# Adding b2 to x with accumulating DMAs in the main loop of a cross-attention and FFN kernel

## The chip, the cores and the metric

The kernel runs on one core of one Trainium2 chip. A core has TensorE (PE; matmuls, with a row of its own, PEld, for weight loads), VectorE (DVE), ScalarE (ACT), GpSimd (POOL) and SyncE (SP), which here only issues DMAs, and 16 DMA engines. The engines run side by side and wait for each other through semaphores; each works off its own queue in order. The metric is the device time of one execution in microseconds. Before the change the median of 3 runs is 529.81 us (529.16 to 530.25).

## The reference

The inputs are x of 4 x 2048 rows of 512, a context of 154 rows per batch, and weights. What matters of the reference, shortened:

```python
x = x + xattn(layernorm(x), ctx, Wq, Wkv, Wout, bout)
x = x + ffn(layernorm(x), w1, b1, w2, b2, gamma, beta)

def ffn(x, w1, b1, w2, b2, gamma, beta):
    h = layernorm(x) * gamma + beta
    h = qlinear(h, w1, b1)
    h = gelu(h)
    return qlinear(h, w2, b2)

def qlinear(x, w, b):
    xq, sx = act_quant(x)      # rows to integers in -128..127
    wq, sw = weight_quant(w)   # the matrix to -1, 0, 1
    return xq @ wq.T / (sx * sw) + b
```

The last bias, b2, is a row of 512 numbers that is added to every row of the output. It can be added anywhere on the way: to the result of the last matrix product, or, as here, to the residual x that the result is added to. The mask of the attention leaves each query few keys or, where none is within the context, the mean of all, so that the attention's part of x comes down to the addition of a few precomputed rows.

## The kernel before

The 8192 rows of x are cut into 64 tiles of 128 rows (the partitions) x 512. Two neighbouring tiles make a pair, which is loaded with one DMA of 512 KB into a buffer of a ring of 12 (`ring`, `load_pair`, L172); `x_of(n)` is one half of it. The order of all work is written out by hand: three strings of words, BEGINNING, STEADY and ENDING, in which a letter names a step and a number a tile. STEADY is one turn of four tiles, and the loop issues it for n = 12, 16, ..., 52, that is for tiles 12 to 55, with the numbers relative to n. Each step puts its instructions at the end of its engines' queues, so the order of words is the order on each engine.

A tile goes through these steps:

- `L` load of the pair (SP); `A`/`a` add the attention's rows to x (L237, GpSimd in the loop).
- `S` row statistics (VectorE, L244 and L245); `N` from them shift and scale for a group of four tiles (eight small GpSimd instructions, L260 to L267); `B`/`K` the normalized tile h (L287 on ScalarE or L294 on GpSimd) and gamma and beta (L299, L300, GpSimd).
- `R` the largest of each row of h (L322, L328, L330, VectorE); `v` two products of four numbers a row, on VectorE (L336, L338); `Q` quantization to float16 integers (L342, ScalarE); `T` a DMA transpose to xqT (L353, SP).
- `I` seeds the PSUM tile `ph` with b1 (L500 VectorE or L502 ScalarE); `U` 16 matmuls on top (L510); `G` gelu (L529, ScalarE), `M` the largest of each row (L541, VectorE, and L555 to L558), `H` quantization (L570, ScalarE), `h` the DMA transpose to hqT (L581, SP), `W` 16 matmuls (L588) into `po`.
- `D` one product per row (L563, GpSimd, after `M`); **`X` adds b2 to x (L316, GpSimd)**; `F` the output tile, po times the scale plus x (L594, VectorE, after `W`, `D` and `X`); `f` its store (L599, SP).

`h` buffers, PSUM tiles and transposed tiles rotate, so a step also waits for the step that last used its buffer: the pair's buffer is free for the next load after `F` of both its tiles.

The first tile of the pair is even. In STEADY, the words of GpSimd stand in this order, with X at four places:

```
U0 ... D-1
U1 ... X0 X1 N8 ... K7 ... K8 ... D0 a14
U2 ... a12 ... D2 D1 a13 ...
U3 X2 ... K9 ... a15 X3 ... K10 ...
```

`F0` stands in U2, `F1` in U3, and `F-2` and `F-1` (of tiles 2 and 3) in the next turn's U0 and U1. In that U0 the words for VectorE and SP run `Q2 F-2 L14 f-2`, and in U1 `R6 T2 h0`: on SP the store of tile 2 stands ahead of the transpose of x of the next turn's third tile. After the turns of n = 12, 28 and 44 the two loads of `second` follow (`s`, L469 and L472), after those of n = 24 a load of `mean` (`t`, L475). The block `b2_b` is b2 copied to all 128 partitions.

Of the kernel before, what the change touches and what calls it, by code (L numbers as in the profile page):

```python
# [41 lines left out]
ALU = mybir.AluOpType  # L42
# [3 lines left out]
P = 128  # L46
# [7 lines left out]
def xattn_ffn(ctx: ExitStack, tc, x, ctxT, WvT, Wout, bout, w1T, b1, w2T, b2, gamma, beta, out):  # L54
    nc = tc.nc
    B, S, D = x.shape
# [5 lines left out]
    NT = B * S // P  # L62
# [19 lines left out]
    FIRST = 12  # L82
# [61 lines left out]
    def constant(shape, dtype, name):  # L144
        return const.tile(shape, dtype, tag=name, name=name)
# [10 lines left out]
    gamma_b, beta_b, b2_b = (constant([P, D], F32, s) for s in ("gamma_b", "beta_b", "b2_b"))  # L156
# [10 lines left out]
    pairs = {}  # L167
# [6 lines left out]
    def x_of(n):  # L174
        return pairs[n // 2][:, n % 2, :]
# [134 lines left out]
    def close_affine(n):  # L310
        g, j = group_of[n]
        h, r = normed[n], rstd[g][:, j : j + 1]
        nc.vector.scalar_tensor_tensor(h, h, r, beta_b, ALU.mult, ALU.add)

    def add_b2(n, e=nc.gpsimd):
        e.tensor_tensor(x_of(n), x_of(n), b2_b, ALU.add)  # L316

    def row_scales(n):
        g, j = group_of[n]
# [287 lines left out]
    def by_half(f):  # L607
# [60 lines left out]
        "D": dequant2,  # L668
        "W": down,
        "X": add_b2,  # L670
        "x": lambda n: add_b2(n, nc.vector),
        "F": finish,
        "f": store,
# [55 lines left out]
```

## Time and profile before

| What | Value |
|---|---|
| median of 3 runs | 529.81 us |
| profiled execution | 528.89 us |
| its span, first to last instruction | 527.1 us |
| granted TensorE clock over the span | 0.992 |
| L510, 1024 matmuls (first product) | 233.5 us busy |
| L588, 1024 matmuls (second product) | 231.2 us busy |
| GpSimd, `h<-h,gamma_b` and `h<-h,beta_b` (L299, L300) | 71.6 and 71.4 us, x56 each |
| GpSimd, `x<-x,mean` (L237) | 69.7 us, x55 |
| x loads: 32 of 512 KB | 4.9 us to landing (median) |
| stores: 64 of 256 KB | 2.8 us to landing |
| transposes hqT: 65 | 4.3 us to landing |
| transposes xqT: 64 | 2.5 us to landing |
| DMA queue of SP | 73.6% of 16 engines' span |

The busy time is the sum over an engine's instructions in one profiled execution. Matmuls overlap, so the busy time of PE is the time in which at least one runs. The DMA engines' share in a stretch is the mean time that packets took, over 16 engines; it can pass 1 where packets overlap. "To landing" counts from the issue of a DMA to its last byte's semaphore. In the lists of the page each group has its line, engine and operation, output and inputs with shapes and count, then busy time and mean, then the idle time of the engine just ahead of it. In a timeline each row has start, length, engine, line and operation.

The changed sums, L316, fall in the loop between 162 and 459 us: tile 12's is at 162.51, tile 55's at 458.06.

### The profile page before, as it was taken

To read this page: it belongs to the slowest core of one execution; us is meant where nothing else is said; L and a number is where in the kernel's file an instruction comes from. 1 tells how busy PE (TensorE), PEld (TensorE's weight loads), DVE (VectorE), ACT (ScalarE), POOL (GpSimd) and SP (SyncE) were. 2 spreads that over 40 slices of the span, in tenths; PEclk is the share of its full clock that TensorE was granted. 3 is DMA by queue.
4 is the path that set the end of the run, shared out by engine and by line. 5 is a ranking of instruction groups with operands and counts; after the bars stand their busy time and mean duration, and the time that the engine had idled before them with its cause. 6 is when DMAs were issued, how large, how long until landed. Compare 5 with 4: busy or idle time off the path is not lost.

```text
span 527.1 us, 6898 instructions
## 1 busy us (share of the span) xinstructions
PE 498.8 (95%) x2164; PEld 222.3 (42%) x2164; DVE 434.8 (82%) x760; ACT 422.4 (80%) x387; POOL 405.4 (77%) x526
## 2 busy tenths in 40 slices
PE   6999848998999999999999999999999999999996
PEld 2444313433444444444444444444444444444442
DVE  1078998998888898989899988999999998787762
ACT  1386876698789888898888879898888888888971
POOL 0045489999999999999999999899999998852220
PEclk9999979999999999999999999999999999999999
DMA  8998066675799797868777696858596956576654
GB/s 305 401 391 304 11 174 134 182 175 141 165 188 202 140 213 157 204 156 187 164 188 167 139 234 145 193 127 206 133 207 139 218 103 158 111 168 132 130 116 125
DMA packets 194112, 94.00 MB, mean 178 GB/s; under 512 B 170268, under 2 KB 170268, under 8 KB 194076
## 3 DMA queue, kind: packets, MB, share of 16 engines
q1 hardware_dynamic: 194076, 93.56, 73.6%
q8 instruction: 17, 0.28, 0.2%
q14 instruction: 19, 0.16, 0.1%
HBM read 34.55 MB, written 17.04 MB: 98 GB/s over the span
## 4 chain that ended last, share of the span: by engine, by line
PE 57%; POOL 16%; DVE 11%; DMA 9%; ACT 3%; issue 3%; SPq 0%; ACTq 0%; POOLq 0%; DVEq 0%
PE ph L510 28%; PE po L588 27%; POOL x L237 4%; DMA xqT<-xqg 3%; DVE m L541 3%; POOL h L300 2%; POOL h L299 2%; POOL x L316 2%; DMA ctx_sb<-ctxT_dram 2%; DVE bn L244 2%; DVE ph L500 1%; DMA ws<-w2T_dram 1%; PE wps L391 1%; DVE o L594 1%; POOL r L261 1%
## 5 line engine op out<-in xcount | busy, mean ns | idle before, releaser
L510 PE MATMUL ph<-w1q,xqT 128*128 128x512 f16 x1024 | 233.5, 381 | 13.4 <-DMA xqT<-xqg 10.0
L588 PE MATMUL po<-w2q,hqT 128*128 128x512 f16 x1024 | 231.2, 379 | 6.0 <-DMA hqT<-hq 6.0
L541 DVE TENSOR_REDUCE m<-hid 128x1 f32<-128x1024 f32 (+1 forms) x130 | 152.9, 1192 | 20.4 <-ACT hid L529 19.9
L529 ACT ACTIVATE hid<-ph,d 128x1024 f32<-128x1024 f32 (+1 forms) x130 | 141.1, 1093 | 24.1 <-PE ph L510 23.2
L570 ACT ACTIVATE hq<-hid,i 128x2048 f16<-128x2048 f32 (+1 forms) x65 | 128.2, 1974 | 39.0 <-issue 19.2
L510 PEld LDWEIGHTS <-xqT 128*128 128x128 f16 x1024 | 99.9, 98 | 138.7 <-DMA xqT<-xqg 15.2
L588 PEld LDWEIGHTS <-hqT 128*128 128x128 f16 x1024 | 99.7, 98 | 128.3 <-DMA hqT<-hq 8.9
L502 ACT ACTIVATE ph<-b_b,inv 128x1024 f32<-128x1024 f32 x81 | 89.9, 1112 | 4.4 <-POOL inv L336 3.4
L316 POOL TENSOR_TENSOR x<-x,b_b 128x512 f32<-128x512 f32 x63 | 80.2, 1283 | 0.0
L299 POOL TENSOR_TENSOR h<-h,gamma_b 128x512 f32<-128x512 f32 x56 | 71.6, 1278 | 5.4 <-ACT h L287 1.2
L300 POOL TENSOR_TENSOR h<-h,beta_b 128x512 f32<-128x512 f32 x56 | 71.4, 1274 | 4.4
L237 POOL TENSOR_TENSOR x<-x,mean 128x512 f32<-128x512 f32 x55 | 69.7, 1275 | 2.8 <-DMA x<-x_dram 2.8
L594 DVE SCALAR_TENSOR_TENSOR o<-po,d,x 128x512 f32<-128x512 f32 x64 | 47.8, 746 | 16.9 <-PE po L588 8.9
L500 DVE TENSOR_SCALAR ph<-b_b,inv 128x1024 f32<-128x1024 f32 x47 | 59.6, 1268 | 1.4 <-POOL inv L336 1.3
L322 DVE TENSOR_REDUCE m<-h 128x1 f32<-128x512 f32 x64 | 43.1, 675 | 6.7 <-POOL h L300 6.6
L342 ACT ACTIVATE xqg<-h,s 128x512 f16<-128x512 f32 x64 | 45.5, 711 | 1.6 <-DVE s L330 1.6
L244 DVE BATCH_NORM_STATS2 bn<-x 128x6 f32<-128x512 f32 x64 | 43.6, 682 | 2.5 <-POOL x L237 2.4
L563 POOL TENSOR_TENSOR d<-mh,wm 128x1 f32<-128x1 f32 x64 | 12.1, 198 | 39.8 <-DVE mh L556 35.9
L294 POOL TENSOR_SCALAR h<-x,rstd,shift 128x512 f32<-128x512 f32 x50 | 38.6, 773 | 0.0
L391 PE MATMUL wps<-wo,wv 128*128 128x512 f32 x64 | 30.9, 645 | 4.2 <-DMA wo<-Wout_dram 4.2
L214 POOL TENSOR_SCALAR w1q<-wi 128x1024 f16<-128x1024 int16 x6 | 6.1, 1035 | 31.8 <-ACT wi L211 31.8
L225 ACT ACTIVATE junk<-ws 128x1024 int16<-128x1024 f32 x10 | 10.5, 1051 | 19.3 <-DMA ws<-w1T_dram 17.9
(74 smaller groups left out, 251.7 us busy)
## 6 DMA issues: line engine op xcount, KB each, us to landing
x<-x_dram SPq DMA_DIRECT2D x32, 512.0 KB, 4.9
out_dram<-o SPq DMA_DIRECT2D x64, 256.0 KB, 2.8
ws<-w1T_dram SPq DMA_DIRECT2D x8, 512.0 KB, 7.2
ws<-w2T_dram SPq DMA_DIRECT2D x8, 512.0 KB
wv<-WvT_dram SPq DMA_DIRECT2D x8, 256.0 KB, 5.9
wo<-Wout_dram SPq DMA_DIRECT2D x8, 256.0 KB, 5.7
ctx_sb<-ctxT_dram SPq DMA_DIRECT2D x1, 1232.0 KB
hqT<-hq SPq DMA_TRANSPOSE x65, 4.3
```

Of the source, the lines that this page charges most:

```text
L237: e.tensor_tensor(x_of(n), x_of(n), y, ALU.add)
L244: nc.vector.bn_stats(st, x_of(n))
L299: nc.gpsimd.tensor_tensor(normed[n], normed[n], gamma_b, ALU.mult)
L300: nc.gpsimd.tensor_tensor(normed[n], normed[n], beta_b, ALU.add)
L316: e.tensor_tensor(x_of(n), x_of(n), b2_b, ALU.add)
L500: nc.vector.tensor_scalar(ph, row, d, None, ALU.mult)
L502: nc.scalar.activation(ph, row, AF.Identity, bias=0.0, scale=d)
L510: nc.tensor.matmul(bank[i], xqT[n][:, k, :], w1q[:, k, i * 512 : (i + 1) * 512], start=False, stop=(k == KD - 1), skip_group_check=True,)
L529: nc.scalar.activation(hidden[n][:, i * w : (i + 1) * w], up_ps[n][half][:, lo : lo + w], AF.Gelu, bias=0.0, scale=deq1[g][:, j : j + 1],)
L541: nc.vector.tensor_reduce(m2[:, i : i + 1], hidden[n][:, i * w : (i + 1) * w], AX.X, ALU.max, apply_absolute_value=True,)
L570: nc.scalar.activation(hq[n][:, lo : lo + w], hidden[n][:, lo : lo + w], AF.Identity, bias=0.0, scale=inv2[n],)
L588: nc.tensor.matmul(po, hqT[n][:, k, :], w2q[:, k, :], start=(k == 0), stop=(k == KH - 1))
```

## The change

In the loop, `add_b2` does nothing for the even tile of a pair. For the odd tile it issues one DMA on GpSimd's queue that adds b2 to both halves of the pair in place: the source is `b2_b` read twice, the destination is the pair. Outside the loop (tiles 0 to 11 and 56 to 63) the sums stay as they were.

```diff
     def add_b2(n, e=nc.gpsimd):
-        e.tensor_tensor(x_of(n), x_of(n), b2_b, ALU.add)
+        if not FIRST <= n < NT - 8:
+            e.tensor_tensor(x_of(n), x_of(n), b2_b, ALU.add)
+        elif n % 2:
+            nc.gpsimd.dma_start(
+                out=pairs[n // 2],
+                in_=b2_b.unsqueeze(1).to_broadcast([P, 2, D]),
+                accum_op=ALU.add,
+            )
```

On GpSimd's queue 44 sums are gone, and 22 DMA issues stand where the sums of tiles 13, 15, ..., 55 stood. In the loop, `F` (L594) now waits for the pair's DMA at the pair's first tile, in place of GpSimd's sum, and the next load into the same buffer waits for that DMA too. All other instructions keep their order on every engine.

## The prediction

> **What bounds the kernel now.** I read the page first, then busy time by stretches of the loop, then the chain of waits and the timeline around each hole in TensorE's row.
>
> ```profile
> PE 498.8 (95%) x2164; PEld 222.3 (42%) x2164; DVE 434.8 (82%) x760; ACT 422.4 (80%) x387; POOL 405.4 (77%) x526
> ...
> L316 POOL TENSOR_TENSOR x<-x,b_b 128x512 f32<-128x512 f32 x63 | 80.2, 1283 | 0.0
> ```
>
> TensorE is busy 95% of the span; the sum of b2 costs GpSimd 1.28 us a tile and no idle time stands before it. The stretches show where TensorE still waits (stretch, length, then busy time and instructions of PE, PEld, DVE, ACT, POOL, then clock, DMA share, GB/s):
>
> ```profile
> 166.00:194.00 28.00, 27.25 (x128) 12.19 (x126) 24.07 (x44) 23.52 (x21) 26.60 (x34) 1.00 0.78 173
> 194.00:304.00 110.00, 109.12 (x506) 49.31 (x505) 98.97 (x173) 95.87 (x85) 104.45 (x131) 1.00 0.78 171
> 304.00:415.00 111.00, 110.03 (x510) 49.72 (x509) 103.12 (x172) 96.03 (x84) 103.82 (x127) 1.00 0.78 174
> 415.00:442.00 27.00, 26.79 (x125) 12.01 (x124) 24.96 (x43) 23.63 (x21) 25.06 (x32) 1.00 0.73 159
> ```
>
> From 166 to 442 us, nearly the whole changed loop, TensorE is idle 0.75 + 0.88 + 0.97 + 0.21 = 2.8 us of 276. It runs at the full granted clock (1.00), 16 matmuls in 3.45 us, a tile in 6.91. So no edit of GpSimd can win more than about 2.8 us, 0.5%. The idle is in three places, 111 us apart: before L510 of tiles 18, 34 and 50, which start 7.95, 8.04 and 7.28 us after the tile before, against 6.91 (holes of 1.04, 1.13 and 0.37). The chain of waits in order of time (start, length, what) shows what ends two of them:
>
> ```profile
> 301.54 6.38 DMA xqT<-xqg
> 307.96 3.63 PE ph L510 x16
> ...
> 413.02 5.79 DMA xqT<-xqg
> 418.86 3.63 PE ph L510 x16
> ```
>
> A transpose of x takes 2.4 us to land at the median of 200 to 440 us; here 6.4 and 5.8, because it queues behind the loads of second, of the next x pair and a store. TensorE waits on a **DMA**, not on GpSimd. GpSimd is nevertheless nearly full: 104.45 of 110 us, and the 5.5 us left are 0.04 us for each of 131 instructions. It keeps pace with a loop that TensorE sets.
>
> **The change, step by step.** The loop covers tiles 12 to 55: 44 sums go, 22 DMAs of GpSimd come, two per turn of four tiles (27.6 us).
>
> *Removed.* 44 x 1.28 = 56 us of GpSimd, 2.57 us a pair. Almost all of it lies beside TensorE's saturated row, so its direct worth is nothing. It is on the path once: in the chain from 165 to 184 us one sum (1.23 us at 179.15) stands among the GpSimd work that leads to the hole of tile 18. It also holds VectorE up: L338, four numbers a row, takes 0.15 us alone, but 1.31 where it starts with the sum (288.48 and 288.50), in the chains to the holes of 34 and 50. Upper worth: all of the holes, 2.5 us. [...] I take **-1.6**: about 0.8 at tile 18, 0.4 at each of the others.
>
> *Added on GpSimd.* The issue of a DMA of 128 rows x 2 pieces with an add. No DMA is issued on GpSimd in this trace. Lower bound: SP's issue of the x load of the same size, 0.40 us. Upper: SP's issue of the largest transpose when the queue holds it up, 4.6 us. I take 1.5, nearest to SP's unhindered issues with many pieces (1.2 for xqT, 1.9 for hqT). Then a pair costs GpSimd 2.57 - 1.5 = 1.07 us less, and the cover holds. The break-even is 2.57; above it GpSimd falls behind a loop in which it has no room.
>
> *Added on the DMA queues.* Each pair reads 512 KB of b2, reads 512 KB of x and writes it back. The page's fastest slice moves 401 GB/s, so one pass of 512 KB takes 1.3 us. [...] 2.6 us a pair, 5.2 a turn, 19% of 27.6. By row alone it would be 1.3 a pair. No row here shows an add, so I take the higher one. The mean DMA share of the loop is 0.78, so this fits on average, but not everywhere. The added DMAs share engines with the transposes, whose slack before TensorE I read from the timeline: for tile 38, issue at 330.11, landing 2.4 later, L510 at 335.60, slack 3.1; for hqT of tiles 44 and 48, 2.5 and 1.7 us; for xqT of tile 30, beside a mean load, 1.3; **for tiles 18, 34 and 50 none**. A delay of up to 2.6 us is thus swallowed in an ordinary turn. At the three tiles it is paid: the second DMA of the turn is issued where the sum pair stood (299.25 us, or some 2 us earlier), just before the loads and the transpose at 301.54. But DMA engines are half empty there for about two microseconds [...], so I take half of 2.6: +1.3 each, **+3.9**. Tile 30: 2.6 less the slack of 1.3, halved likewise: **+0.7**.
>
> *Added wait.* L594 now waits for the DMA's landing. It stands in VectorE's queue ahead of L244, the hidden maximum L541 and the seeding L500, and its store stands on SP just ahead of the next xqT. The tightest place is the second pair of a turn:
>
> ```profile
> 233.81 1.28 POOL L316 TENSOR_TENSOR x<-x,b_b 128x512 f32<-128x512 f32 x1
> ...
> 239.74 1.27 POOL L316 TENSOR_TENSOR x<-x,b_b 128x512 f32<-128x512 f32 x1
> ...
> 244.87 0.75 DVE L594 SCALAR_TENSOR_TENSOR o<-po,d,x 128x512 f32<-128x512 f32 x1
> ```
>
> The sum at 233.81 goes, so the DMA can be issued at 239.74 - 1.28 = 238.5; the sum of the output needs it at 244.9: 6.4 us (7.2 for tile 30). [...] By the row nearest in size, the x load, 512 KB: 4.9 us at the median in this traffic, plus 1.3 for the second read, plus 1.5 of issue = 7.7, late by 1.3. [...] A lateness of 1.3 us delays the store and the transpose behind it, which has 3.1 us of slack in ordinary turns; at tiles 34 and 50 the budget is 7.2 to 7.4 us, so 0.3 to 0.5 late, within the delay already counted (the same transpose waits for both). Cost taken: 0; bounds 0 and, at a landing of 11 us, (11 - 6.4 - 3.1) = 1.5 a turn, 16 over 11 turns. The waits of the x loads and of L237 for the old buffers' DMAs cost nothing: L594 has read those buffers by then.
>
> **Sum.** -1.6 + 3.9 + 0.7 = +3.0 on the profiled execution's 528.9 (span 527.1), 531.9. That run lies 0.9 below the median of 529.8, so for a median: **532.5**, own range 531 to 537. About 0.2%, 1.06 us, is what a measurement can tell from no change.
>
> **Rivals.**
> 1. *The holes shrink* (25%). The added DMAs fall into the half-empty stretches, land in 3 to 5 us, and the sum's relief reaches the three holes: -2.0 of the possible 2.5: 527.8. [...] Against it: the holes end with a DMA, in the traffic to which the change adds.
> 2. *GpSimd becomes the bound* (15%). If the issue takes 3.5 us, a pair costs 0.93 more, a turn 1.9; some 0.4 a turn of room, then 1.5 x 11 = 16: 546. It decides from an issue of 2.6 us on; at the upper bound, 4.6 us, it would be 2.0 a pair, (4.1 - 0.4) x 11 = 40 us, which I leave outside the range. For it: no free time on POOL from 100 to 440 us; against it: the size of SP's issues.
> 3. *The DMA lands too late everywhere* (10%): 11 us, 1.5 a turn: 546. It decides from 6.4 + 3.1 = 9.5 us on.
> 4. *Nothing to tell* (12%): everything lies in slack: 529.8.
> The forecast keeps 38%. That the change does not what it says: the order of the other instructions is unchanged on all engines, so no.
>
> **How the numbers follow.** Faster: rival 1, and a small tail of the forecast in which half of the holes close: 0.27. Same: 0.11. Slower: 0.62. The range goes from 527.5 (all holes gone, 529.8 - 2.5, rounded) to 546 (rivals 2 and 3).
>
> **What would show it.** Right: POOL about 23 us lower; its DMA rows near 1.5 us; TensorE's stretches 194 to 304 and 304 to 415 idle 1 to 3 us more each, all before tiles 18, 30, 34 and 50, with xqT as releaser and landings of 7 us or more there; in other turns 6.91 us a tile. Rival 1: those holes below 0.5 us and L338 at 0.15. Rival 2: POOL rows of DMA over 2.6 us, and TensorE waiting in every turn with POOL in the chain. Rival 3: L594 waiting for the accumulating DMA by over 3 us in every turn. I am wrong in kind if TensorE loses time in ordinary turns, or in the tail after 442 us, which the change doesn't touch.

## The result and the profile after

The changed kernel takes 565.34 us (median of 4 runs, 561.08 to 567.73) beside 529.68 us: 1.066 times as long, 95% interval 1.060 to 1.073. The profiled execution took 565.13 us, with a span of 563.4 us. One run below, of the moved DMAs, is over 1.5% above the fastest of its kernel, at a lower clock, and is left out. In its listing all lines behind `add_b2` stand 8 lower: L510 became L518, L588 L596, L353 L361, L581 L589, L594 L602.

The page of the changed kernel, first the busy times, then the queues of the DMAs (packets, MB, share of 16 engines' span) and GpSimd's issues:

```profile
PE 509.9 (91%) x2164; PEld 223.2 (40%) x2164; DVE 425.8 (76%) x760; ACT 424.2 (75%) x387; POOL 377.8 (67%) x504
...
q1 hardware_dynamic: 194076, 93.56, 70.7%
q0 software_dynamic: 5984, 11.54, 12.1%
...
L320 POOL DMA_DIRECT2D x<-b_b x22 | 27.2, 1236 | 0.0
```

GpSimd did get lighter, from 405.4 to 377.8 us, and an issue costs it 1.24 us in place of 2.57 for the two sums. All the time is lost elsewhere. The same stretches as before the change, in the same columns:

```profile
166.00:194.00 28.00, 22.85 (x96) 9.77 (x95) 18.99 (x35) 19.22 (x18) 22.11 (x28) 0.88 0.86 147
194.00:304.00 110.00, 99.49 (x450) 43.65 (x449) 85.02 (x150) 84.46 (x74) 82.19 (x107) 0.98 0.95 194
304.00:415.00 111.00, 104.60 (x473) 46.03 (x471) 90.12 (x162) 89.70 (x78) 84.00 (x106) 0.98 0.93 190
415.00:442.00 27.00, 26.08 (x121) 11.64 (x121) 22.24 (x42) 22.86 (x20) 22.13 (x27) 1.00 0.93 200
```

TensorE is now idle for 5.2, 10.5, 6.4 and 0.9 us, every other engine is busy for less of each stretch than before, and the DMA share, 0.73 to 0.78 before, is 0.86 to 0.95. In the view of all waits TensorE's own are these (engine and line waited for whom, us in total, times, longest):

```profile
PE ph L518 <- DMA xqT<-xqg: 32.9, 14, 5.7
...
PE po L596 <- DMA hqT<-hq: 10.4, 14, 3.4
```

Before, they were:

```profile
PE ph L510 <- DMA xqT<-xqg: 10.0, 7, 5.6
PE po L588 <- DMA hqT<-hq: 6.0, 6, 2.7
```

The transposes arrive late: in the stretch from 150 to 500 us an xqT lands 4.1 us after its issue (median) in place of 2.5, an hqT 4.7 in place of 4.3, at most 8.3 in place of 6.2. VectorE's output sum L602 has no wait for the new DMA among those that the profile shows before it.

The turns of the loop, from L510 (L518) of their first tile to that of the next turn's, in us:

| tiles | before | after | more |
|---|---|---|---|
| 12 to 15 | 28.6 | 35.2 | 6.7 |
| 16 to 19 | 28.7 | 34.8 | 6.1 |
| 20 to 23 | 27.6 | 29.4 | 1.7 |
| 24 to 27 | 27.6 | 28.9 | 1.3 |
| 28 to 31 | 27.6 | 30.8 | 3.2 |
| 32 to 35 | 28.8 | 33.7 | 5.0 |
| 36 to 39 | 27.6 | 29.6 | 2.0 |
| 40 to 43 | 27.6 | 28.7 | 1.1 |
| 44 to 47 | 27.6 | 28.9 | 1.3 |
| 48 to 51 | 28.0 | 34.8 | 6.8 |
| 52 to 55 | 27.6 | 28.2 | 0.6 |

That sums to 35.6 us, the whole loss. In each turn it stands before the third tile (14, 18, ..., 54), and in four turns also before the tile behind that. By the starts of the matmuls from tile 12 on, gaps between two of them grew by 28 us, and a second part, 7 us, is matmuls at half speed: before the change, 1 of them started more than 0.35 us (and less than 0.6) after the one ahead, after the change 35 did. Windows around the late tile 34 show why; the figure behind the five engines is the granted clock:

```profile
323.00:331.00 8.00, 3.93 (x18) 1.60 (x18) 5.85 (x11) 4.73 (x4) 7.30 (x11) 0.99 1.00 204
331.00:334.40 3.40, 3.40 (x9) 1.20 (x8) 0.00 (x0) 0.00 (x0) 2.86 (x4) 0.52 0.99 229
334.40:341.00 6.60, 6.60 (x32) 3.02 (x31) 4.75 (x10) 5.54 (x5) 1.90 (x4) 1.00 0.71 164
```

TensorE waits for 4 us, and then the clock is 0.52 for 3.4 us: 9 matmuls in place of 16. The stall costs 1.7 us more than its own length. The same happens after the four longest waits of the loop (3.7, 4.4, 5.1 and 5.2 us), three times for 3.4 us and once for 6.8; after the next longest, 2.3 us, it doesn't. The length of the wait alone doesn't tell: in runs below, waits of 2.4 us (second pair's DMA alone, at 429 us) and of 2.0 us (`v` on GpSimd, at 170 us) were followed by half the clock too. The prediction didn't count this.

**What the DMA engines do meanwhile.** For the stretch before tile 34, the shares of the 16 engines that packets of SP's queue and of GpSimd's queue took, by microsecond, from the packets of the trace:

```
from us    SP's queue   GpSimd's queue
313        0.00         0.58
314        0.03         1.09
315        0.17         0.96
316        0.57         0.46
317        1.04         0.00
318        1.21         0.00
319        1.18         0.00
320        0.44         0.72
321        0.03         1.12
322        0.14         1.02
323        0.82         0.02
```

Here the queues take turns: for some 3 us the adding DMA has the engines, and SP's queue all but stands. Of the 22 adding DMAs, 20 took 2.8 to 3.5 us from the first packet to the last, and SP's packets took 0.10 to 0.18 of the engines meanwhile. The other two shared more: 6.8 us with SP's packets at 0.44 (the loop's first), and 4.1 us at 0.35. A packet of the add, 2048 bytes, takes 178 ns where one of that size on SP's queue takes 84 (medians); all packets of one DMA make 3.1 us of all 16 engines. SP's own issues then stall as well. SP's queue ahead of the late transpose, before:

```profile
296.38 2.08 SPq L581 DMA_TRANSPOSE hqT<-hq  x1
298.55 0.81 SPq L599 DMA_DIRECT2D out_dram<-o  x1
299.41 0.41 SPq L469 DMA_DIRECT2D second<-rest_dram  x1
299.87 0.29 SPq L472 DMA_DIRECT2D second<-rest_dram  x1
...
301.54 1.41 SPq L353 DMA_TRANSPOSE xqT<-xqg  x1
```

and the same DMAs after:

```profile
315.21 3.96 SPq L589 DMA_TRANSPOSE hqT<-hq  x1
319.27 0.90 SPq L607 DMA_DIRECT2D out_dram<-o  x1
320.21 1.29 SPq L477 DMA_DIRECT2D second<-rest_dram  x1
321.55 1.17 SPq L480 DMA_DIRECT2D second<-rest_dram  x1
...
323.87 1.73 SPq L361 DMA_TRANSPOSE xqT<-xqg  x1
```

The issue of hqT takes 3.96 in place of 2.08 us, those of second 1.2 to 1.3 in place of 0.3 to 0.4. Counted from L510 of tile 33 (299.93 before, 319.50 after), the transpose that tile 34 waits for is issued at 4.4 in place of 1.6 us. Most of what tile 34 loses, 3.3 us, is this late issue; its landing took 6.9 in place of 6.4 us.

### The profile page after: what moved, and what is told of

The parts are those of the page before. It is cut to its first block, busy times and chain, and to the rows that moved or that the text cites. A ratio compares the mean times of both kernels' runs of the same rounds, so it can differ in the third digit from the quotient of the medians.

```text
span 563.4 us, 6904 instructions
## 1 busy us (share of the span) xinstructions
PE 509.9 (91%) x2164; PEld 223.2 (40%) x2164; DVE 425.8 (76%) x760; ACT 424.2 (75%) x387; POOL 377.8 (67%) x504
## 4 chain that ended last, share of the span: by engine, by line
PE 57%; DMA 19%; POOL 12%; DVE 6%; ACT 2%; issue 2%; SPq 1%; ACTq 0%; POOLq 0%; DVEq 0%
PE ph L518 32%; PE po L596 25%; DMA xqT<-xqg 11%; POOL x L237 3%; DMA hqT<-hq 2%; POOL x L318 2%; DMA ctx_sb<-ctxT_dram 2%; POOL h L300 2%; POOL h L299 2%; DVE m L549 1%; DMA ws<-w1T_dram 1%; DMA ws<-w2T_dram 1%; DMA wv<-WvT_dram 1%; ACT hid L537 1%; POOL r L261 1%
## 5 line engine op out<-in xcount | busy, mean ns | idle before, releaser
L518 PE MATMUL ph<-w1q,xqT 128*128 128x512 f16 x1024 | 240.2, 389 | 33.3 <-DMA xqT<-xqg 32.9
L596 PE MATMUL po<-w2q,hqT 128*128 128x512 f16 x1024 | 233.0, 381 | 10.5 <-DMA hqT<-hq 10.4
L549 DVE TENSOR_REDUCE m<-hid 128x1 f32<-128x1024 f32 (+1 forms) x130 | 155.1, 1197 | 64.4 <-ACT hid L537 63.0
L518 PEld LDWEIGHTS <-xqT 128*128 128x128 f16 x1024 | 101.2, 100 | 164.9 <-DMA xqT<-xqg 40.1
L596 PEld LDWEIGHTS <-hqT 128*128 128x128 f16 x1024 | 99.4, 98 | 136.4 <-DMA hqT<-hq 18.0
L578 ACT ACTIVATE hq<-hid,i 128x2048 f16<-128x2048 f32 (+1 forms) x65 | 128.2, 1974 | 30.4 <-issue 11.5
L510 ACT ACTIVATE ph<-b_b,inv 128x1024 f32<-128x1024 f32 x81 | 89.9, 1112 | 4.4 <-POOL inv L344 3.4
L602 DVE SCALAR_TENSOR_TENSOR o<-po,d,x 128x512 f32<-128x512 f32 x64 | 47.7, 746 | 25.8 <-PE po L596 18.5
L294 POOL TENSOR_SCALAR h<-x,rstd,shift 128x512 f32<-128x512 f32 x50 | 43.4, 868 | 0.0
L399 PE MATMUL wps<-wo,wv 128*128 128x512 f32 x64 | 30.8, 644 | 4.2 <-DMA wo<-Wout_dram 4.2
L260 POOL TENSOR_SCALAR a<-mv 128x4 f32<-128x4 f32 (+2 forms) x17 | 3.3, 192 | 37.9 <-DVE mv L245 37.4
L320 POOL DMA_DIRECT2D x<-b_b x22 | 27.2, 1236 | 0.0
```

The costliest lines, as they stand in the source:

```text
L510: nc.scalar.activation(ph, row, AF.Identity, bias=0.0, scale=d)
L518: nc.tensor.matmul(bank[i], xqT[n][:, k, :], w1q[:, k, i * 512 : (i + 1) * 512], start=False, stop=(k == KD - 1), skip_group_check=True,)
L549: nc.vector.tensor_reduce(m2[:, i : i + 1], hidden[n][:, i * w : (i + 1) * w], AX.X, ALU.max, apply_absolute_value=True,)
L578: nc.scalar.activation(hq[n][:, lo : lo + w], hidden[n][:, lo : lo + w], AF.Identity, bias=0.0, scale=inv2[n],)
L596: nc.tensor.matmul(po, hqT[n][:, k, :], w2q[:, k, :], start=(k == 0), stop=(k == KH - 1))
L602: nc.vector.scalar_tensor_tensor(rows_out[n], down_ps.pop(n), deq2[n], x_of(n), ALU.mult, ALU.add)
```

## The experiments

The theory: the bytes of the added DMAs hold up the transposes of SP's queue, and TensorE waits for those. The rivals: GpSimd's issue, the output sum's wait for the landing, and the queueing behind the loads of `second`. The ratios below are to the kernel before, run on the same chip, with their 95% intervals.

**Nothing in the loop.** In the loop, b2 isn't added at all:

```diff
         elif n % 2:
-            nc.gpsimd.dma_start(
...
+            pass
```

> Leaves out the addition of b2 in the loop (tiles 12 to 55): neither the sums nor the DMAs. Traffic theory (the added DMAs hold up the transposes of SP's queue): 527 to 529 us, as GpSimd has less to do and nothing is added. If GpSimd's lost place in the order, the freed GpSimd running ahead, or anything but the added DMAs is the cause, it stays well above 535 us.

526.94 us, ratio 0.9938 (0.9916 to 0.9960). Without the sums the kernel is 0.6%, some 3.3 us, faster. All that the change could have won is this, and the new order of work loses nothing. In its trace the holes of tiles 18 and 50 are gone, that of tile 34 went from 1.1 to 0.7 us, and a fourth, of tile 14, from 0.9 to 0.2.

**The same DMAs, but short.**

```diff
-                out=pairs[n // 2],
-                in_=b2_b.unsqueeze(1).to_broadcast([P, 2, D]),
+                out=pairs[n // 2][:, :, :8],
+                in_=b2_b[:, :8].unsqueeze(1).to_broadcast([P, 2, 8]),
```

> Leaves out most of the addition of b2 in the loop: each of the 22 DMAs has its 256 pieces, but of 32 bytes in place of 2048. Traffic theory: 527 to 531 us, since the bytes are gone. Issue theory [...]: 555 to 565 us. Wait theory (the output's sum waits for the landing): below 540 us[...].

528.52 us, 0.9982 (0.9962 to 1.0001). GpSimd's issues are as long as in the changed kernel:

```profile
L320 POOL DMA_DIRECT2D x<-b_b x22 | 27.2, 1235 | 0.0
```

27.2 us on GpSimd, the same number of packets, landings after 4.1 us (median) in place of 6.6, and no loss: neither the issue nor the pieces cost the time. The bytes do.

**The same DMAs into a buffer that nobody reads** (a part of the context's tile, which is free by then):

```diff
-                out=pairs[n // 2],
+                out=scratch[n // 2 % 2],
```

> Leaves out the addition of b2 in the loop: the same 22 accumulating DMAs add b2 to a spare buffer that nobody reads, so the output's sum and the x loads wait for none of them. Traffic theory: 560 to 568 us, as with the change. Wait theory: 528 to 535 us.

566.41 us, 1.068 (1.063 to 1.073), as with the change. The output sum's wait and the wait of the x loads are not the cause.

**Plain copies in place of adds**, one and then two for each pair, into such buffers:

```diff
-                out=pairs[n // 2],
+                out=scratch[n // 2 % 2],
                 in_=b2_b.unsqueeze(1).to_broadcast([P, 2, D]),
-                accum_op=ALU.add,
```

> Leaves out the addition of b2 in the loop: 22 plain copies of b2, 512 KB each, on GpSimd's queue into a spare buffer that nobody reads. If the cost is the second read and the slow packets of the add (178 ns in place of 85), the copies hold the DMA engines 1.4 in place of 3.0 us: 535 to 545 us. If any DMA of GpSimd's queue holds up the transposes for as long: 555 to 565 us.

533.87 us, 1.007 (1.004 to 1.010). A copy took 1.54 us of all engines, half of an add, in packets of 4096 bytes. Eight of the 22 had the engines nearly to themselves (SP's packets took 0.02 to 0.13 meanwhile), the others shared them (0.19 to 0.54). The loss is a little less than expected.

> Leaves out the addition of b2 in the loop: two plain copies of 512 KB per pair on GpSimd's queue, 44 in all, into two spare buffers. They hold the DMA engines about as long as the adds, 2 x 1.55 us against 3.05. If engine time in such stretches is what costs: 552 to 568 us. If an add is worse than a copy of the same engine time, since SP's queue gets no share beside it: 537 to 550 us.

557.37 us, 1.055 (1.050 to 1.059): within what engine time predicts, and outside the other range. Two copies of 1.48 us, one behind the other, cost some 24 us more than one, each counted from the kernel before on its chip. With the loss counted from the 526.94 without either, two copies (2.96 us a pair) cost 30 us, an add (3.1 to 3.2) 38 to 40. Engine time explains most of an add's cost; why an add costs 8 to 10 us more for 0.1 to 0.2 us more of it a pair is open. **The cost isn't in proportion**: 1.54 us a pair cost 7.

**One DMA per turn**, the other pair by sums as before: first the second pair's alone, then the first pair's.

```diff
-        if not FIRST <= n < NT - 8:
+        if not FIRST <= n < NT - 8 or n % 4 < 2:
```

> Only the second pair of each turn (tiles 2 and 3) is added by a DMA, 11 DMAs; the first pair by GpSimd's sums as before. If each DMA costs the same (engine time is simply used up), 530 + 36/2 = 548 us. If one stretch of 3 us per turn still fits into the transposes' slack, and only two together go over it: 533 to 542 us.

541.15 us, 1.022 (1.020 to 1.025): 11.5 us.

> Only the first pair of each turn (tiles 0 and 1) is added by a DMA, the second by GpSimd's sums. The run with the second pair alone cost 11.5 us. If the two DMAs of a turn act each for itself: 36 - 11.5 = 24.5, 554 us. If it is the two together that go over the transposes' slack, each alone is cheap: 536 to 545 us.

549.62 us, 1.040 (1.035 to 1.046): 20.5 us, between the two expectations. The two make 32 of 35.7, so most of the loss is each DMA's own, and the idea that two together are needed falls. The place matters: the first pair's DMA costs nearly twice as much. In the trace of the changed kernel it is the one that runs just ahead of the transpose of the turn's third tile, which had 3.1 us of slack or none. Taking turns is not what makes it dear: alone, nine of its eleven DMAs shared the engines, for 4.7 to 8.0 us with SP's packets at 0.49 to 0.70, and the loss was there all the same.

**The same bytes in shorter stretches**: a DMA for each tile.

```diff
-        elif n % 2:
-            nc.gpsimd.dma_start(
-                out=pairs[n // 2],
...
+        else:
+            nc.gpsimd.dma_start(out=x_of(n), in_=b2_b, accum_op=ALU.add)
```

> 44 DMAs of one tile each, in the places of the 44 sums, in place of 22 of a pair: the same bytes in stretches of about 1.5 us in place of 3.0. If the length of an unbroken stretch decides, since a transpose that arrives meanwhile waits for its end: 545 to 556 us. If only the bytes count: 562 to 568 us. GpSimd's issue becomes 44 x 1.2 us, still no more than the sums.

552.03 us, 1.044 (1.039 to 1.050), as expected of stretch length, though the 44 DMAs took more engine time (1.81 us each, 3.6 a pair). A third of the loss is gone with more traffic; that the bytes alone count falls. That the length decides is likely but not shown: the first tile's DMA also starts earlier than the pair's did, so the place changed too.

**Moved.** In STEADY, the first DMA goes behind `N8`, the second ahead of `a15`:

```diff
-        U1 S11 H0 I2.0.1 G1.0 R6 T2 h0 G1.1 Q3 M1.0 X0 X1 I2.1.0 N8 W-1 K7 T3 M1.1 F-1 K8
+        U1 S11 H0 I2.0.1 G1.0 R6 T2 h0 G1.1 Q3 M1.0 I2.1.0 N8 X0 X1 W-1 K7 T3 M1.1 F-1 K8
...
-        U3 X2 G3.0 I4.0.0 G3.1 S13 K9 I4.1.0 W1 Q5 T5 a15 X3 M3.0 f0 M3.1 H3 K10 h3 R9 F1
+        U3 X2 G3.0 I4.0.0 G3.1 S13 K9 X3 I4.1.0 W1 Q5 T5 a15 M3.0 f0 M3.1 H3 K10 h3 R9 F1
```

> The first DMA of a turn stands behind the eight small instructions of the group's norms, 3.5 us later, the second one step of 1.3 us earlier, ahead of the addition of the attention's rows: the two are then some 8 in place of 5 us apart on GpSimd. Traffic theory: the place decides, the time moves by more than 5 us, to 545 to 558 us if they fall between the transposes better. If only the sum of engine time counts: 562 to 568 us.

560.84 us (three runs, 554.06 to 562.23), 1.056 (1.048 to 1.064). Neither expectation was met in the sum. In the trace nine of the eleven turns lose 3.0 us together, where they lost 22.7 with the change, and two, of tiles 16 and 48, lose 13.2 and 15.6: in each of the two an hqT landed late, 17.7 and 19.2 us after its issue. So the place decides in both directions; why these two turns stall is open.

**The loads of second elsewhere**, in the changed kernel, and then in the kernel before:

```diff
+    do("s1")
     for n in range(FIRST, NT - 8, 4):
         do_all(STEADY, n)
-        if n % TB == 12:
+        if n % TB == 4 and n // TB + 1 < B:
             do(f"s{n // TB + 1}")
```

> The changed kernel with the loads of second taken from the turns of tiles 18, 34 and 50 to earlier turns. If those turns lose 5 to 7 us each because the adding DMAs meet these loads there: 550 to 557 us. If the transposes would be late there without them: 560 us or more.

561.33 us, 1.060 (1.058 to 1.062), 4 us below the change, so by the time alone the loads would seem not to matter. The trace says otherwise: the turns of tiles 18, 34 and 50 take 28.8, 29.0 and 29.8 us in place of 34.8, 33.7 and 34.8, and the turns in which the loads now stand, of tiles 14, 26 and 42, take 38.5, 31.6 and 33.5 in place of 35.2, 28.9 and 28.7. The first three together win 15.7 us, the others lose 10.7 of it again. So the large losses stand where the adds meet these loads.

> The kernel before, with the loads of second taken to earlier turns, so that the transposes of tiles 18, 34 and 50 don't queue behind them: the holes of 1.0, 1.1 and 0.4 us close for two thirds or more, 528.0 to 528.8 us beside 529.7. If the holes come from VectorE's wait for GpSimd's sums instead: no change beyond 0.1%.

530.61 us, 1.0024 (1.0006 to 1.0042), slightly slower: a miss. Here too the holes moved with the loads. In the trace tiles 18, 34 and 50 start 6.9 us after the tile before, without a hole; holes stand at tile 42, 0.5 us, at tile 14, 1.8 in place of 0.9, both just behind the moved loads, and at tile 30, 1.0 where there was none, behind a load of `mean`. At tile 42:

```profile
356.82 0.40 SPq L469 DMA_DIRECT2D second<-rest_dram  x1
357.28 0.32 SPq L472 DMA_DIRECT2D second<-rest_dram  x1
...
359.09 1.23 SPq L353 DMA_TRANSPOSE xqT<-xqg  x1
...
365.10 1.25 PE L510 MATMUL ph<-w1q,xqT 128*128 128x512 f16 x5 [0.38 <-DMA xqT<-xqg]
```

> As the run before, and the two products of the group's scales (v, VectorE, held up to 1.3 us by GpSimd's sums) go to GpSimd. If VectorE's wait is the rest of the holes: 527.0 to 528.3 us. If GpSimd, which has no free time, falls behind by 0.5 us a turn: above 530 us.

```diff
-        U2 I3.0.1 G2.0 h1 R7 M2.0 G2.1 Q4 M2.1 I3.1.0 W0 a12 L16 D2 D1 a13 R8 F0 T4 v4 S12
+        U2 I3.0.1 G2.0 h1 R7 M2.0 G2.1 Q4 M2.1 I3.1.0 W0 a12 L16 D2 D1 a13 R8 F0 T4 V4 S12
```

530.64 us, 1.0025 (1.0012 to 1.0037), a miss too. No version that adds b2 everywhere was faster than the kernel before. The prediction's reading, that the holes come of the loads of `second` ahead of a transpose, fits the trace with the loads moved; leaving the sums out closed or shrank the same holes, so the sums have a part. How the two share them, and what the products add, stays open.

**By turns.** From one trace of each kernel, the time of each turn less that of the kernel before, in us:

| tiles | one copy a pair | second pair's add | first pair's add | both (the change) | moved | loads elsewhere |
|---|---|---|---|---|---|---|
| 12 to 15 | 1.1 | -0.6 | 6.6 | 6.7 | -0.6 | 9.9 |
| 16 to 19 | 0.7 | 5.6 | 0.9 | 6.1 | 13.2 | 0.2 |
| 20 to 23 | 0.0 | 0.0 | 0.9 | 1.7 | 0.0 | 1.6 |
| 24 to 27 | 0.0 | 0.0 | 1.0 | 1.3 | 1.4 | 3.9 |
| 28 to 31 | 0.7 | 1.5 | 2.5 | 3.2 | 2.1 | 3.2 |
| 32 to 35 | -0.1 | 0.8 | 0.9 | 5.0 | 0.1 | 0.2 |
| 36 to 39 | 0.0 | 0.0 | 0.7 | 2.0 | 0.0 | 1.2 |
| 40 to 43 | 0.1 | 0.0 | 0.0 | 1.1 | 0.0 | 5.8 |
| 44 to 47 | 0.0 | 0.0 | 1.7 | 1.3 | 0.1 | 1.1 |
| 48 to 51 | 2.0 | 3.9 | 4.1 | 6.8 | 15.6 | 1.8 |
| 52 to 55 | 0.0 | 0.0 | 0.0 | 0.6 | 0.0 | 0.6 |

A copy a pair, or the second pair's add alone, costs the six ordinary turns (of tiles 20, 24, 36, 40, 44 and 52) 0.1 us at most: the delay goes into the transposes' slack. The first pair's add goes over it in four of them, both adds in all six.

## Why the prediction was wrong

The direction was right, for the reason forecast, transposes that land late; the size was not: +3.0 us on the profiled execution, and it became +36.2; 565 lies above the range.

- **What bounds the kernel**: right. TensorE's row is what the loop's time follows, GpSimd's relief is worth little. The relief was put at 1.6 us, at most 2.5; leaving the sums out measured 3.3 (2.1 to 4.5). That only a part of VectorE's delay would go was my estimate: L338 took 1.30 to 1.31 us at five of its 13 places before, L346, the same line after, 0.15 at all 13, ten of them beside L294. One hole was misread: the 0.75 us of the first stretch (166 to 194 us) is not tile 18's but a fourth hole's, of tile 14. The four make 3.5 us.
- **GpSimd's issue**: taken as 1.5 us, measured 1.24. Rival 2 is out.
- **The added wait**: taken as nothing, and right. The landing was put at 7.7 us from the x load's row; the profile gives 6.6 in this traffic. Rival 3 needed 9.5 us and more; the spare buffer shows that the wait costs nothing.
- **The engine time of an add**: taken as 2.6 us a pair, an estimate of mine of two passes of 1.3 at the page's 401 GB/s; measured 3.1. A copy's 1.54 agrees with the 1.3 of one pass roughly, so here an add did take twice a copy.
- **The step that failed** is the one after it, the delay of the transposes: "A delay of up to 2.6 us is thus swallowed in an ordinary turn. At the three tiles it is paid", halved for the half-empty stretch, +3.9, and +0.7 at tile 30. Against the tile before, tiles 18, 34 and 50 start 4.5, 3.3 and 5.1 us later than they did, in place of 1.3 each, and tile 30 3.2 in place of 0.7; with the slow clock behind them, the turns of these four lost 21.1 us of the 35.6, but 4.6 were counted. The rest fell where nothing was counted: 6.7 in the turn of tiles 12 to 15 and 0.6 to 2.0 in each ordinary turn. Three things were wrong in the term:
  1. The delay was taken as half of one DMA's engine time. SP's issues stall behind an add as well: before tile 34 the transpose is issued 2.8 us later. And only one DMA of a turn was counted, the one at the place of the sum pair. It is called the second; in the order of words it is the first pair's. Both cost time, 11.5 and 20.5 us alone. That an add would fill half-empty engines (busy for 0.39 and 0.60 of the two microseconds from 301 us before) did not hold for most DMAs of the changed kernel; where the queues did share, with the first pair's alone, the loss stayed.
  2. Slack does swallow a delay, as the table by turns shows, but not that of both adds: the six ordinary turns lost 7.9 us. The turn of tiles 12 to 15 I had left out: tile 14 started 7.8 us after tile 13 before the change, so its transpose had no slack either, and now starts 12.2 after.
  3. After each of the four longest waits TensorE ran at half its clock: 7 of the 36 us, not priced at all.
- **The mean DMA share** of 0.78 from which I argued that the traffic fits was the wrong figure. It leaves 6.1 us a turn, and the two adds took 6.2; and even where traffic fits on average, a transpose with a deadline meets the stretch that happens to run.

## What to carry to other kernels

An engine without idle time need not be the bound: here, beside a saturated TensorE, GpSimd's sums were worth 0.6%, and what replaced them had to cost less than that. Before work is moved to DMAs, list the transfers that TensorE waits for and their slack one by one, and hold against each the engine time of all new DMAs near it, with the issues that stall behind them (here 3.1 us an add, and before tile 34 a transpose issued 2.8 us later), not their share on average. If TensorE may stall by some microseconds, add the slow clock after the stall (here, after a wait of 3.7 us, 3.4 us at 0.52, which cost 1.7). And where an edit moves a transfer, compare turn by turn: the same total can hide a loss that only changed its place.

## What was not expected of the hardware

- In the changed kernel DMAs of GpSimd's queue and of SP's queue mostly took turns by microseconds: 20 of 22 adds left SP's packets 0.10 to 0.18 of the engines. And the other way round: of a turn's two DMAs one had its first packet 1.8 us after its issue, the other, issued into a running transpose, 3.8. It is no fixed rule: with one add a turn, of the first pair, nine of eleven shared the engines with SP's queue. What decides between the two is not known.
- An adding DMA's packets of 2048 bytes took 178 ns, a copy's of 4096 bytes 165, and those of 32 bytes, in the short DMAs, 27.
- Loss against engine time bends up: 1.5 us a pair cost 7 us, 3.0 cost 30. The table by turns shows why: the ordinary turns pay only when their slack is used up.
